# Making the scan's input for four of sixteen units with ScalarE and TensorE instead of VectorE and GpSimd

## The chip, the cores and the metric

The kernel runs on one core of one Trainium2 chip. The core has TensorE (PE in the profile), VectorE (DVE), ScalarE (ACT), GpSimd (POOL), and SyncE (SP), which here only issues DMAs. The metric is the device time of one launch in microseconds. Times are in us unless marked otherwise.

## What is computed

The first of two layers takes `x` of shape (8, 64, 128, 128), runs a small Mamba block along every row and along every column, in both directions, and adds the four results; the second is a residual block of two 3x3 convolutions with batch normalisation. Nearly all the time goes to the Mamba part. Cut to what matters, for one sequence of 128 tokens, 128 inner channels `d` and 16 states `n`:

```python
x, z  = in_w @ seq                                    # 64 -> 128 + 128 channels
u     = silu(causal_conv4(x))                         # four taps along the sequence
dt, B, C = xp_w @ u                                   # 4 + 16 + 16 values per token
delta = softplus(dt_w @ dt + dt_b)
h[d, n] = exp(delta[d] * A[d, n]) * h[d, n] + (delta[d] * u[d]) * B[n]    # per token, in order
y[d]  = sum_n h[d, n] * C[n] + u[d] * D[d]
out   = out_w @ (y * silu(z))
```

The line with `h` is the heavy one: 128 x 16 recurrences for every sequence and direction, so 2048 per token, against 128 lanes in an engine.

## The kernel before

**Groups and units.** The work is cut into 512 groups (8 images, rows then columns, 32 groups each; a group is four sequences, 512 tokens). The recurrences of a group are cut into 16 units. A unit is one direction `d`, one set of four states `ng`, and one half of the channels: 32 channels x 4 states on the 128 partitions, and two channel quarters x 512 tokens along the free axis, 128 x 1024 in all. `where(r)` gives direction, state set and half of unit `r`. For every unit:

- `decay` (L360): ScalarE writes exp(A * delta), two ACTIVATEs of 128x512, into one of two PSUM tiles, `dA0` for even units and `dA1` for odd ones. So a decay can only start when the scan two units earlier has read the same PSUM tile.
- `drive` (L369): delta*u*B, a 128x1024 product. For 11 units VectorE makes it from `du` and `pb`, a PSUM tile in which TensorE has spread B over the partitions (`b_rows`, L353); for the five units in `GPS` GpSimd makes it, from a copy of B fetched by DMA (`b_tile`).
- `scan` (L377): VectorE runs the recurrence along the tokens, in the tile `s`.
- `weigh` (L386): GpSimd multiplies by C.
- `add_up` (L399): TensorE sums over the states into PSUM, four units later.

`s` comes from a pool of eight tiles. `pb`, `bp` and `zp` share one PSUM bank (tag `b`); `cp`, `dp`, `op` and others share one two-bank slot (tag `pt`).

**The order.** No scheduler moves anything: the loop over `s` at the end of the function writes every engine's instruction order by hand, and each engine runs its own queue in that order. One turn of the loop is one unit `r`. Into these turns the loop lays, piece by piece, `prepare` for the next group: four taps of the convolution as matmuls (L237 for rows, L243 for columns), `u` (Silu, L268), `dp` (L275), `bp` and its copy `bc` (L280, L285), softplus (L290), `du` on VectorE and `dl` on ScalarE (L302, L304, and L306, which overwrites each sequence's first or last token), then DMAs that write `du` and `dl` to memory and read them back in the units' layout (`replicate`, L328). Silu and softplus each need another ScalarE table than Exp, so every group loads tables four times. At fixed turns come `gate` (`y`, L412), `emit` (the output product and its copy), and, for the previous image, `normalize` and the first convolution `conv1`.

All DMAs of this part are issued from SP's queue in one order. Images are held whole in SBUF (`xt`); columns are read out of it by a ScalarE copy (L255).

Of the kernel before, what the change touches and what calls it, by code (L numbers as in the profile page):

```python
# [15 lines left out]
P = 128  # L16
# [4 lines left out]
SEQ = N // W  # L21
NCH = W // SEQ
# [7 lines left out]
GPS = (2, 5, 9, 12, 15)  # L30
# [3 lines left out]
def tile_mamba2d_then_resblock(ctx: ExitStack, tc: tile.TileContext, x, par, gn, p_w, o_w, new_p, bn, cst, out):  # L34
# [32 lines left out]
    with tc.tile_pool(name="prep", bufs=2) as prep, tc.tile_pool(name="prep_ps", bufs=2, space=PSUM) as prep_ps:  # L67
        iv = ident.rearrange("p (c n) -> p n c", n=4)
# [3 lines left out]
        for o, p in enumerate(par):  # L72
# [6 lines left out]
            wc = const.tile([P, 2, NTAP, P], F32, name=f"wc{o}")  # L79
            wz = const.tile([P, 2, P], F32, name=f"wz{o}")  # L80
            nc.vector.memset(wc, 0.0)
            nc.vector.memset(wz, 0.0)
            for hf in range(2):
                h = slice(hf * C, (hf + 1) * C)
                for j in range(NTAP):
                    nc.vector.tensor_mul(wc[h, hf, j, :], inw[h, 0:P], cw[h, j, :])
                nc.vector.tensor_copy(wz[h, hf, :], inw[h, P : 2 * P])
# [13 lines left out]
            wb = const.tile([P, NG, 32, 4], F32, name=f"wb{o}")  # L101
            for g in range(NG):
                nc.vector.tensor_copy(
                    wb[:, g], xpT[:, 4 + 4 * g : 8 + 4 * g].unsqueeze(1).to_broadcast([P, 32, 4])
                )
# [3 lines left out]
            av = p["A_log"].rearrange("(q c) (g n) -> q g c n", c=32, n=4)  # L109
# [12 lines left out]
            for hf in range(2):  # L122
# [7 lines left out]
                    wc=wc, wz=wz, wd=wd, wb=wb.rearrange("p g c n -> p (g c n)"), wbc=xpT[:, 4:], A=A, wo=wo,  # L130
# [75 lines left out]
    with ExitStack() as st:  # L206
# [9 lines left out]
        xt = big.tile([P, HH, W], F32, name="xt")  # L216
        xp = big.tile([P, HH, W], F32, name="xp")
        strips = []
        for k in range(2):
            strip = big.tile([P, SEQ + 1, W + 2], F32, name=f"strip{k}")  # L220
            nc.vector.memset(strip, 0.0)
            strips.append(strip)
        far = big.tile([P, SEQ], F32, name="far")
        nc.vector.memset(far, FAR)

        def load_image(b, k):

            rows = slice(k * (HH // 8), (k + 1) * (HH // 8))
            nc.sync.dma_start(out=xt[:, rows, :], in_=x[b].rearrange("p (h w) -> p h w", w=W)[:, rows, :])

        def project(ps, lhsT, g, s, start, stop):

            ps = ps.rearrange("p (q t) -> p q t", t=W)
            if g["o"] == 0:
                hf, r = divmod(SEQ * g["i"], HH)
                lo, hi = max(s, 0), W + min(s, 0)
                nc.tensor.matmul(  # L237
                    ps[:, :, lo:hi], lhsT[hf], xt[:, r : r + SEQ, lo - s : hi - s], start=start, stop=stop
                )
                return  # L240
            for hf in range(2):
                lo, hi = max(hf * HH + s, 0), min((hf + 1) * HH + s, W)
                nc.tensor.matmul(  # L243
                    ps[:, :, lo:hi], lhsT[hf], g["xc"][:, :, lo - s - hf * HH : hi - s - hf * HH],
                    start=start and hf == 0, stop=stop and hf == 1, skip_group_check=True,
                )

        def prepare(g, before):
# [3 lines left out]
            if g["o"] == 1:  # L252
                g["xc"] = work.tile([P, SEQ, HH], F32, name="xc", bufs=1)
                i = SEQ * g["i"]
                nc.scalar.copy(g["xc"], xt.rearrange("p h w -> p w h")[:, i : i + SEQ, :])  # L255
            yield
            cp = psm.tile([P, 2, N], F32, name="cp", tag="pt")
            for d in range(2):
                for s in range(NTAP):
                    j = NTAP - 1 - s  # L260
                    project(
                        cp[:, d, :], [w["wc"][:, 0, j, :], w["wc"][:, 1, j, :]], g,
                        s if d == 0 else -s, s == 0, s == NTAP - 1,
                    )
                    if s % 2:
                        yield
# [10 lines left out]

            bp = psa.tile([P, N], F32, name="bp", tag="b")
            for d in range(2):
                nc.tensor.matmul(  # L280
                    bp[2 * NS * d : 2 * NS * (d + 1), :], w["wbc"], u[:, d, :], start=True, stop=True,
                    skip_group_check=True,
                )
            bc = work.tile([4 * NS, N], F32, name="bc", tag="tok", bufs=3)
            nc.scalar.copy(bc, bp[0 : 4 * NS, :])  # L285
            bd = scratch.tile([2 * NS, 2, N], F32, name="bd")
            nc.sync.dma_start(out=bd.rearrange("n d t -> d n t"), in_=bc)
            g["bd"] = bd
# [11 lines left out]

            du = work.tile([P, 2, N], F32, name="du", tag="nat")
# [3 lines left out]
            for d, edge in enumerate((0, W - 1)):  # L305
                nc.scalar.copy(dl[:, d, :].rearrange("p (s t) -> p s t", t=W)[:, :, edge], far)  # L306
            keep(1, du)
            keep(0, dl)
            yield
            replicate(g, 0, 0)  # L310
            yield
            replicate(g, 1, 0)
            yield
            replicate(g, 0, 1)
            yield
            zp = psa.tile([P, N], F32, name="zp", tag="b")
            project(zp, [w["wz"][:, 0, :], w["wz"][:, 1, :]], g, 0, True, True)
            g["sz"] = work.tile([P, N], F32, name="sz")
            nc.scalar.copy(g["sz"], zp)
            replicate(g, 1, 1)  # L320
            yield

        def replicate(g, half, d):

            for k, what in enumerate(("dl", "du")):
                t = rep.tile([P, 2, N], F32, name=what, bufs=5)
                src = g["dd"][k, d, :, 2 * half : 2 * half + 2, :].rearrange("c q t -> c (q t)")
                nc.sync.dma_start(  # L328
                    out=t.rearrange("p q t -> p (q t)"), in_=src.unsqueeze(1).to_broadcast([32, 4, 2 * N])
                )  # L330
                g[what, half, d] = t

        def where(r):

            ng, k = divmod(r, 4)
            return k % 2, ng, k // 2

        def c_rows(g, r):
# [4 lines left out]
            nc.sync.dma_start(out=t, in_=src.partition_broadcast(32))  # L343
            g["c", ng, d] = t

        def b_tile(g, r):

            half, ng, d = where(r)
            t = rep.tile([P, N], F32, name="bt", bufs=3)
            nc.sync.dma_start(out=t, in_=g["bd"][4 * ng : 4 * ng + 4, d, :].partition_broadcast(32))  # L350
            g["bt", r] = t
# [8 lines left out]
        def decay(g, r):  # L360

            half, ng, d = where(r)
            dA = g["dA", r] = psa.tile([P, 2, N], F32, name=f"dA{half}")
# [5 lines left out]
        def drive(g, r):  # L369
# [3 lines left out]
            engine, b = (nc.gpsimd, g.pop(("bt", r))) if r in GPS else (nc.vector, g["pb"])  # L373
            engine.tensor_mul(s, g["du", half, d], b.unsqueeze(1).to_broadcast([P, 2, N]))  # L374
            g["s", r] = s

        def scan(g, r):  # L377
            half, ng, d = where(r)
            a = g.pop(("dA", r)).rearrange("p j t -> p (j t)")
            s = g["s", r].rearrange("p j t -> p (j t)")  # L380
            if d == 0:
                nc.vector.tensor_tensor_scan(s, a, s, 0.0, ALU.mult, ALU.add)  # L382
            else:
                nc.vector.tensor_tensor_scan(s[:, ::-1], a[:, ::-1], s[:, ::-1], 0.0, ALU.mult, ALU.add)  # L384
# [29 lines left out]
        def emit(g):  # L414

            o, i, w = g["o"], g["i"], wt[g["o"]]
            op = psm.tile([P, 2, N], F32, name="op", tag="pt")[:, 0, :]
# [97 lines left out]

        PREP = range(14)
# [3 lines left out]
        LOAD = (2, 4, 6, 8)  # L522
# [8 lines left out]
        def fetch(s):  # L531

            for k in range(10):
                r = (s + k) % UN
                if 0 <= s + k < total and r in GPS and k == {GPS[0]: 9, GPS[1]: 4}.get(r, 7):
                    b_tile(*at(s + k))
                if 0 <= s + k < total and r % 2 == 0 and k == {0: 7, 4: 4}.get(r, 5):
                    c_rows(*at(s + k))

        def ahead(r):  # L540

            return 2 if r == GPS[0] else 3

        with tc.manual_schedule():
            for k in range(8):
                load_image(0, k)
            for _ in prepare(gs[0], None):
                pass
            for s in range(-9, 0):
                fetch(s)  # L550
            decay(*at(0))
            b_rows(*at(0))
            drive(*at(0))
            for s in range(total + UN):
                n, r = divmod(s, UN)
                live = n < len(gs)
                prev = gs[n - 1] if n else None
                if r == 0:
                    for _ in pieces:
                        pass  # L560
                    pieces = prepare(gs[n + 1], gs[n]) if n + 1 < len(gs) else iter(())
                if s + 1 < total:
                    decay(*at(s + 1))
                    if (s + 1) % UN not in GPS:
                        drive(*at(s + 1))
                for k in (2, 3):
                    if s + k < total and (s + k) % UN in GPS and ahead((s + k) % UN) == k:
                        drive(*at(s + k))
                if live:
                    scan(*at(s))  # L570
                    weigh(*at(s))
                if r == LAG - 1 and prev:
                    gate(prev)
                if s == total - 1:
                    nc.scalar.activation(gs[n]["sz"], gs[n]["sz"], AF.Silu)
                if s % 2 == 0 and s + 2 < total:
                    b_rows(*at(s + 2))
                if r in CONV and n % PER > 6 or r >= CONV[0] and n % PER == 6:
                    next(conv3, None)
                if r in PREP:  # L580
# [177 lines left out]
```

## Time and profile before

| | |
|---|---|
| median of three runs | 27018.82 us (27011.33 to 27033.64) |
| the profiled execution, its own time | 27039.83 us |
| span of its profile | 27038.1 us |
| VectorE busy | 25627.1 us, 95% of the span |
| GpSimd busy | 25129.4 us, 93% |
| TensorE busy | 19439.9 us, 72% |
| ScalarE busy | 17413.3 us, 64% |
| DMA queues, mean rate | 180 GB/s |
| mean granted TensorE clock | 0.876 |

Busy time is the time in which an engine has some instruction in flight. Neighbouring instructions overlap a little, so their durations add up to more than the time they occupy: on VectorE a product lasts 1196 ns by its mean and the next instruction starts about 1.11 us after it. Where instructions follow closely, the distance between starts is the honest price, and the timeline view gives it. "Idle before" in a group's line is the time in which the engine did nothing just before such an instruction, followed by what ended it.

### The profile page before, as it was taken

How to read it: one execution, taken by the hardware profiler on the slowest of the kernel's cores; microseconds unless marked ns; L12 is line 12 of the kernel's file. 1: busy time of each engine (PE TensorE's matmuls, PEld its weight loads, DVE VectorE, ACT ScalarE, POOL GpSimd, SP SyncE). 2: the span in 40 equal slices, each digit the busy share in tenths (PEclk: the TensorE clock that was granted, in tenths of full speed). 3: DMA queues.
4: the chain of work that ended last, by engine and by line, in shares of the span. 5: the costliest groups of instructions: out<-in, count | busy, mean ns of one | idle time of the engine just before them, and what ended most of it. 6: DMA issues, size and time to landing. Idle time of an engine off the chain costs nothing.

```text
span 27038.1 us, 228528 instructions
## 1 busy us (share of the span) xinstructions
PE 19439.9 (72%) x65580; PEld 6680.4 (25%) x65580; DVE 25627.1 (95%) x15633; ACT 17413.3 (64%) x23982; POOL 25129.4 (93%) x10916
## 2 busy tenths in 40 slices
PE   5677777777777777777777777777777777777776
PEld 1222222222222222222222222222222222222232
DVE  8999999999999999999999999999999999999942
ACT  5666666666666666666666666666666666666632
POOL 7999999999999999999999999999999999999930
PEclk8888888888988889888898888988888888988888
DMA  5554555555555555555555555555555555555545
GB/s 181 174 179 172 185 189 184 176 173 186 192 181 175 173 189 192 180 172 173 193 188 177 175 178 193 184 178 174 177 199 179 180 172 182 198 176 179 171 141 188
DMA packets 2165508, 4870.74 MB, mean 180 GB/s; under 512 B 265856, under 2 KB 413456, under 8 KB 2148368
## 3 DMA queue, kind: packets, MB, share of 16 engines
q1 hardware_dynamic: 2143648, 4754.51, 51.8%
q10 hardware_dynamic: 15984, 68.06, 0.9%
q0 software_dynamic: 4608, 33.56, 0.3%
q8 instruction: 517, 8.47, 0.1%
q14 instruction: 751, 6.15, 0.1%
HBM read 4115.52 MB, written 738.98 MB: 180 GB/s over the span
## 4 chain that ended last, share of the span: by engine, by line
DVE 35%; PE 22%; issue 20%; DMA 10%; ACT 10%; SPq 2%; POOL 1%; DVEq 0%; POOLq 0%; ACTq 0%
DVE s L374 15%; DMA du<-dd 9%; DVE s L384 8%; DVE s L382 8%; PE pb L357 6%; ACT dA L365 5%; PE yp L405 5%; PE dp L275 3%; PE cps L667 2%; DVE du L302 2%; PE op L423 1%; PE op L418 1%; PE bp L280 1%; DVE y L412 1%; ACT xp L436 1%
## 5 line engine op out<-in xcount | busy, mean ns | idle before, releaser
L389 POOL TENSOR_TENSOR s<-s,c 128x1024 f32<-128x1024 f32 x8192 | 19136.2, 2362 | 677.1 <-DVE s L384 309.6
L365 ACT ACTIVATE dA<-dl,A 128x512 f32<-128x512 f32 x16384 | 11265.2, 691 | 6399.1 <-DVE s L384 3848.6
L357 PE MATMUL pb<-u,wb 128*128 128x512 f32 x8192 | 5429.6, 750 | 6527.7 <-DVE s L374 5829.9
L384 DVE TENSOR_TENSOR_SCAN s<-dA,s 128x1024 f32<-128x1024 f32 x4096 | 9278.0, 2275 | 15.7 <-POOL s L374 2.5
L382 DVE TENSOR_TENSOR_SCAN s<-dA,s 128x1024 f32<-128x1024 f32 x4096 | 9274.8, 2274 | 0.0
L374 DVE TENSOR_TENSOR s<-du,pb 128x1024 f32<-128x1024 f32 x5632 | 6736.8, 1196 | 168.9 <-DMA du<-dd 100.8
L374 POOL TENSOR_TENSOR s<-du,bt 128x1024 f32<-128x1024 f32 x2560 | 6061.9, 2368 | 142.9 <-DMA bt<-bd 140.8
L405 PE MATMUL yp<-s,fold 128*32 128x512 f32 x32768 | 5170.7, 708 | 5.1 <-POOL s L389 5.1
L357 PEld LDWEIGHTS pb<-u,wb 128*128 128x128 f32 x8192 | 1517.7, 218 | 9607.2 <-issue 3926.7
L237 PE MATMUL cp<-xt,wc 128*128 128x512 f32 (+3 forms) x4096 | 2017.6, 616 | 101.3 <-DMA xt<-x_h 76.9
L243 PE MATMUL cp<-xc,wc 128*128 128x256 f32 (+3 forms) x8192 | 2065.5, 397 | 0.0
L243 PEld LDWEIGHTS cp<-xc,wc 128*128 128x128 f32 x8192 | 1584.7, 199 | 1030.8 <-issue 459.6
L405 PEld LDWEIGHTS yp<-s,fold 128*32 128x32 f32 x32768 | 691.0, 116 | 3773.0 <-issue 1930.8
L365 ACT ACT_TABLE_LOAD x1030 | 1321.5, 1283 | 18.2
L237 PEld LDWEIGHTS cp<-xt,wc 128*128 128x128 f32 x4096 | 764.9, 197 | 1402.0 <-issue 1242.3
L275 PE MATMUL dp<-u,wd 128*128 128x512 f32 x2048 | 1048.9, 638 | 1.2 <-ACT u L268 1.2
L395 PE MATMUL yp<-u,dg 128*128 128x512 f32 x2048 | 963.7, 593 | 1.7 <-DVE y L412 1.7
L696 POOL DMA_DIRECT2D out<-cc x32 | 17.2, 537 | 980.7 <-ACT cc L695 980.7
L436 ACT COPY xp<-op 64x256 f32<-64x256 f32 x512 | 318.2, 621 | 943.2 <-PE op L423 940.2
L495 PE MATMUL cps<-strip,w 128*128 128x512 f32 x1536 | 782.5, 638 | 47.9 <-DMA strip<-x_d 39.4
L418 PE MATMUL op<-y,wo 128*128 128x512 f32 x1024 | 808.7, 882 | 0.8 <-DVE y L412 0.8
L667 PE MATMUL cps<-xp,w 128*128 128x512 f32 x1536 | 675.3, 598 | 8.3 <-ACT xp L655 7.5
(109 smaller groups left out, 10041.2 us busy)
## 6 DMA issues: line engine op xcount, KB each, us to landing
dl<-dd SPq DMA_DIRECT2D x2048, 512.0 KB
du<-dd SPq DMA_DIRECT2D x2048, 512.0 KB
c<-bd SPq DMA_DIRECT2D x4096, 256.0 KB
bt<-bd SPq DMA_DIRECT2D x2560, 256.0 KB
dd<-du SPq DMA_DIRECT2D x2048, 128.0 KB
dd<-dl SPq DMA_DIRECT2D x2048, 128.0 KB
bd<-bc SPq DMA_DIRECT2D x512, 128.0 KB
c_d<-cs SPq DMA_DIRECT2D x256, 256.0 KB
```

The source lines that it names most:

```text
L237: nc.tensor.matmul(ps[:, :, lo:hi], lhsT[hf], xt[:, r : r + SEQ, lo - s : hi - s], start=start, stop=stop)
L243: nc.tensor.matmul(ps[:, :, lo:hi], lhsT[hf], g["xc"][:, :, lo - s - hf * HH : hi - s - hf * HH], start=start and hf == 0, stop=stop and h ...
L275: nc.tensor.matmul(dp[:, d, :], w["wd"], u[:, d, :], start=True, stop=True)
L357: nc.tensor.matmul(pb, wt[g["o"]]["wb"][:, P * ng : P * (ng + 1)], g["u"][:, d, :], start=True, stop=True)
L365: nc.scalar.activation(dA[:, j, :], g["dl", half, d][:, j, :], AF.Exp, scale=wt[g["o"]]["A"][:, 2 * half + j, ng : ng + 1])
L374: engine.tensor_mul(s, g["du", half, d], b.unsqueeze(1).to_broadcast([P, 2, N]))
L382: nc.vector.tensor_tensor_scan(s, a, s, 0.0, ALU.mult, ALU.add)
L384: nc.vector.tensor_tensor_scan(s[:, ::-1], a[:, ::-1], s[:, ::-1], 0.0, ALU.mult, ALU.add)
L389: nc.gpsimd.tensor_mul(s, s, c.unsqueeze(1).to_broadcast([P, 2, N]))
L405: nc.tensor.matmul(g["yp"][32 * q : 32 * (q + 1), :], fold, s[:, j, :], start=False, stop=r == UN - 2, skip_group_check=True,)
L418: nc.tensor.matmul(op, w["wo"].rearrange("p h c -> p (h c)"), g["y"], start=True, stop=o == 0)
L667: nc.tensor.matmul(ps[:, j, :].rearrange("p (r w) -> p r w", w=W), w2[:, blk, kw, :], xp[:, r : r + SEQ, kw : kw + W], start=(kw == 0 and ...
```

## The change

**Order and kinds.** A table `ORDER` gives each of the 16 units its state set, direction and kind. Eight are V (drive on VectorE), four G (drive on GpSimd), four T. Halves still alternate with the unit's number. Units of the same state set and direction share one `pb` (four `b_rows` to a group instead of eight) or one B tile (two `b_tile`s instead of five).

**T units** (4, 7, 12 and 15). Four transposes turn `du` of direction 0 so that tokens lie on the partitions (`duT`), and four small products give B in the same layout (`BT`). `spread` then multiplies: for each state set (2 or 3) and each sequence, four ScalarE activations of 128x128, each with one column of `BT` as its per-partition scale, fill a tile `X`; 32 such activations to a group. `turn` brings the result back with eight TensorE transposes of 128x128 into the PSUM tile `dA0` or `dA1` of that unit. The decay of a T unit goes to an `s` tile in SBUF instead, one to three turns ahead (`EARLY`), and the scan takes its factor from `s` and its input from PSUM.

**Taps.** The image is stacked on the partitions twice, shifted by one token, so that one product does two taps: four matmuls of 128x512 to a group for rows and columns alike, and one for `zp`.

**Columns.** Instead of the whole image, blocks of 32 columns are loaded; a ScalarE copy picks four columns, and DMAs lay them into the stack.

**Layout and places.** The partition order in a unit becomes state-major instead of channel-major, in the constants and in the DMA patterns alike. Within `prepare`, `bp`, `bc` and the `bd` write come later (with `du` and `dl`), and `zp` comes first. All else in the computation is as it was.

```diff
-GPS = (2, 5, 9, 12, 15)
+ORDER = (
+    (0, 0, "V"), (0, 0, "V"), (1, 0, "G"), (1, 0, "G"), (2, 0, "T"), (0, 1, "V"), (0, 1, "V"), (2, 0, "T"),
+    (1, 1, "V"), (1, 1, "V"), (2, 1, "G"), (2, 1, "G"), (3, 0, "T"), (3, 1, "V"), (3, 1, "V"), (3, 0, "T"),
+)
...
+        def spread(g, ng, q):
+            t = g["X", ng, q] = work.tile([P, NQ, 4, 32], F32, name="X", bufs=4)
+            for n in range(4):
+                k = 8 * q + 4 * (ng - TG) + n
+                nc.scalar.activation(
+                    t[:, :, n, :], g["duT"][:, q, :].rearrange("p (q c) -> p q c", c=32), AF.Copy,
+                    scale=g["BT"][:, k : k + 1],
+                )
...
         def decay(g, r):
             half, ng, d = where(r)
-            dA = g["dA", r] = psa.tile([P, 2, N], F32, name=f"dA{half}")
+            if ORDER[r][2] == "T":
+                dA = g["s", r] = unit.tile([P, 2, N], F32, name="s")
+            else:
+                dA = g["dA", r] = psa.tile([P, 2, N], F32, name=f"dA{half}")
...
+        def turn(g, r):
+            half, ng, d = where(r)
+            dB = g["dB", r] = psa.tile([P, 2, N], F32, name=f"dA{half}")
+            for j in range(2):
+                for q in range(SEQ):
+                    nc.tensor.transpose(
+                        dB[:, j, W * q : W * (q + 1)],
+                        g["X", ng, q][:, 2 * half + j, :, :].rearrange("p n c -> p (n c)"), ident,
+                    )
...
+        EARLY = {2: 4, 3: 7, 10: 12, 12: 15}
+        SPREAD = {14: [(2, 0)], 15: [(2, 1)], 0: [(2, 2)], 1: [(2, 3)], 6: [(3, 0)], 7: [(3, 1)], 10: [(3, 2), (3, 3)]}
+        AHEAD = {15: 3, 0: 3, 7: 3, 8: 3}
+        ROWS = {14: 0, 3: 5, 6: 8, 11: 13}
...
+                kind = ORDER[(r + 1) % UN][2]
+                if kind == "T" and live:
+                    turn(*at(s + 1))
+                if g := after if r >= 14 else this:
+                    for k in SPREAD.get(r, ()):
+                        spread(g, *k)
+                if r in EARLY and live:
+                    decay(this, EARLY[r])
+                if kind != "T" and s + 1 < total:
+                    decay(*at(s + 1))
+                if kind == "V" and s + 1 < total:
+                    drive(*at(s + 1))
+                if r in AHEAD and s + AHEAD[r] < total:
+                    drive(*at(s + AHEAD[r]))
                 if live:
-                    scan(*at(s))
-                    weigh(*at(s))
+                    scan(this, r)
+                    weigh(this, r)
```

## The prediction, made before the changed kernel ran

> **What bounds the kernel now.** I read the page's busy times and costliest groups first, then the `y` instructions (one to a group), then the timeline of one row group, engine by engine. From the page:
>
> ```profile
> PE 19439.9 (72%) x65580; PEld 6680.4 (25%) x65580; DVE 25627.1 (95%) x15633; ACT 17413.3 (64%) x23982; POOL 25129.4 (93%) x10916
> ...
> L389 POOL TENSOR_TENSOR s<-s,c 128x1024 f32<-128x1024 f32 x8192 | 19136.2, 2362 | 677.1 <-DVE s L384 309.6
> L365 ACT ACTIVATE dA<-dl,A 128x512 f32<-128x512 f32 x16384 | 11265.2, 691 | 6399.1 <-DVE s L384 3848.6
> ...
> L384 DVE TENSOR_TENSOR_SCAN s<-dA,s 128x1024 f32<-128x1024 f32 x4096 | 9278.0, 2275 | 15.7 <-POOL s L374 2.5
> ...
> L374 DVE TENSOR_TENSOR s<-du,pb 128x1024 f32<-128x1024 f32 x5632 | 6736.8, 1196 | 168.9 <-DMA du<-dd 100.8
> L374 POOL TENSOR_TENSOR s<-du,bt 128x1024 f32<-128x1024 f32 x2560 | 6061.9, 2368 | 142.9 <-DMA bt<-bd 140.8
> ```
>
> VectorE never waits for its scans (15.7 us in all) and hardly for its products: it is the bound, GpSimd just below. ScalarE idles 6399 us before its decays, waiting for scans, 12.5 us to a group. From the `y` line:
>
> ```profile
> L412 DVE TENSOR_TENSOR y<-yp,sz x512: 655/661/692, 188.7 to 25914.2; 128x512 f32<-128x512 f32 x171
> ```
>
> Head 188.7, 511 periods of (25914.2 - 188.7)/511 = 50.34, tail 1124. VectorE's timeline gives the prices:
>
> ```profile
> 9999.27 1.19 DVE L374 TENSOR_TENSOR s<-du,pb 128x1024 f32<-128x1024 f32 x1
> 10000.38 2.28 DVE L382 TENSOR_TENSOR_SCAN s<-dA,s 128x1024 f32<-128x1024 f32 x1
> 10002.58 1.19 DVE L374 TENSOR_TENSOR s<-du,pb 128x1024 f32<-128x1024 f32 x1
> ```
>
> From start to start a product takes 1.11 and a scan 2.20 (`du` 1.12 and `y` 0.58 in the same view). A row group is 16 x 2.20 + 11 x 1.11 + 1.12 + 0.58 = 49.11; the other 1.23 of the period are statistics of columns and convolution, the wait for the column copy (228.8 us in the view of waits, 0.45 a group), image changes. ScalarE's prices, in its timeline:
>
> ```profile
> 9999.38 1.42 ACT L365 ACTIVATE dA<-dl,A 128x512 f32<-128x512 f32 x2 [1.36 <-DVE s L382]
> 10000.82 1.28 ACT L268 ACT_TABLE_LOAD   x1
> 10002.11 1.11 ACT L268 ACTIVATE u<-cp,conv_b 128x1024 f32<-128x1024 f32 x1
> 10003.12 0.62 ACT L270 ACTIVATE sz<-sz 128x512 f32<-128x512 f32 x1
> 10003.64 0.81 ACT L454 ACTIVATE xp<-xp,b_gn,s_gn 128x512 f32<-128x512 f32 x1
> 10004.47 1.28 ACT L365 ACT_TABLE_LOAD   x1
> 10005.76 2.75 ACT L365 ACTIVATE dA<-dl,A 128x512 f32<-128x512 f32 x4
> ```
>
> By starts: a decay 1.44, a table 1.29, `u` 1.01. The first line also shows that a decay starts 0.11 after the scan two units earlier is done.
>
> **What the Trainium skill says.** "ScalarE: Activation LUTs", section "What ACT_TABLE_LOAD costs": an activation takes 186 ns + 0.833 ns per element, each pointer operand adds 93 ns, neighbours overlap by 93 ns. With a pointer scale and 512 elements that is 705; the trace has 691, so I trust it. A `spread` (128 elements, pointer scale) is then an estimated 186 + 93 + 107 = 386 ns, 0.29 from start to start. "TensorE: Matmul & The Clock Gate", "Part 4: PE-mode transpose": about 275 ns for one 128x128 transpose inside a kernel; no run here shows one yet. The same page, "Part 1: The HAM clock gate", says that TensorE's clock halves after a few us of idling; here the `pb` pair takes 1.12 or 2.08:
>
> ```profile
> 10017.29 2.08 PE L357 MATMUL pb<-u,wb 128*128 128x512 f32 x2 [5.92 <-DVE s L374]
> ...
> 10022.78 1.12 PE L357 MATMUL pb<-u,wb 128*128 128x512 f32 x2 [0.32 <-DVE s L374]
> ```
>
> **The change part by part.** VectorE loses three products: 3 x 1.11 = 3.33 a group, to 45.78. GpSimd loses one drive: 20 x 2.34 = 46.8 against 49.1. A T scan swaps which input is in PSUM; I take the same 2.20 (a recurrence paced by its elements), bounds 2.1 and 2.4. TensorE loses four `b_rows` (4 x 1.12) and more than half of the taps, and gains 36 transposes at 0.1 to 0.4, taken as 0.2: in sum no more work than before, so only its waits count. ScalarE gains 32 spreads (32 x 0.30 = 9.6 a group) and two copies (0.48 and some 0.15); T decays write SBUF and lose the wait of the second half for the first, 1.26 instead of 1.44. DMAs: three B tiles fewer, two to four small stack transfers more, column blocks in pieces; engines at a mean share near 53%, all needed a group later. SP's C tile for unit 5 waits at turn 15 for GpSimd's unit 15, and what is behind it (C of unit 8, the stack) is wanted six turns later: nothing. Sharing `dA0`/`dA1` between decays and transposes adds no PSUM but puts a T unit's transposes behind the scan two units earlier.
>
> ScalarE's 9.6 seem to fit in its 12.5 of idling. They don't, because of where they stand. In the changed program ScalarE's queue, from the decay of unit 6 (which waits for scan 4, whose transposes sit in `dA0`) to the decay of unit 11, is fixed. By starts:
>
> decay 6: 1.44; table, `u`, `sz`: 1.29 + 1.01 + 0.64; eight spreads 2.40; table 1.29; decays 8 and 9 2.77; table, softplus, table: 1.29 + 1.11 + 1.29; decay 10 1.44; `dl` 1.04, edges 0.20, `bc` 0.48; eight spreads 2.40; decay 12 (T, ahead of time) 1.26; decay 11 1.42. Sum 22.8, with the start 22.9; 18.1 of it are not spreads.
>
> In that stretch VectorE has scans 5 to 10, drives 6, 8 and 9, and `du`: 6 x 2.20 + 3 x 1.11 + 1.12 = 17.65. So scan 11 must wait 22.9 - 17.65 = 5.2 us for its decay (a part of it, under 1, already at scan 10). Nothing else covers it: scan 11 stands in order on VectorE, and drive 13, scan 12 and GpSimd's unit 11 stand behind it.
>
> The other stretch, from scan 11 to the end of the next group's scan 4, is VectorE's: 10 x 2.20 + 5 x 1.11 + 0.58 = 28.13. ScalarE's work there, 7 decays, 3 T decays, 16 spreads and copies, is near 21 and keeps up. But `b_rows` stands in TensorE's queue behind `turn`: for drive 0, transposes start after scan 13, take 8 x 0.2 = 1.6, then `pb` 1.12 to 2.08 (after the long wait mostly cold) and two hand-overs of 0.1, about 3.4, while VectorE is back after one scan, 2.20: 1.2 late. Drive 5, behind turn 4, has 2.78 (scan, `y`) and is late only when cold: 0.2 on average. (Drive 8 is late too, inside the first stretch, where it costs nothing; without that cover 1.2.)
>
> A group: 22.9 + 28.13 + 1.4, plus `normalize` in a quarter of the groups, 0.83 in the first stretch, 0.2; plus 1.23 - 0.45 = 0.8 of rest: 53.4. Total 188.7 + 511 x 53.4 + 1124 = 28,600 against this profile's 27,039.83; the median shown is 21 less, so 28,580; I say 28,600, 5.8% slower.
>
> **The rivals.** (1) *Faster*: the spreads issue far closer together, and TensorE's turns are never late. For it, the two edge copies of four elements stand 0.1 apart; against it, a pointer scale and 124 more elements. At 0.1 the first stretch is 18.1 + 1.6 = 19.7, a group 19.7 + 28.13 + 1.0 = 48.8, in all 26,260. It decides below a spacing of about 0.19; at 0.2 a group is 50.4, all 27,080: *no change*. (2) *TensorE is late*: transposes at 0.4, clock mostly halved. Drive 0 waits 3.2 + 2.08 + 0.2 - 2.2 = 3.3, drive 5 2.7, and the third set of spreads, which needs the fifth transpose of turn 7, 1.1: 59 a group, 31,400. Against it: 72% busy shrinks rather than grows, and only a quarter of the `pb` pairs were slow. (3) *GpSimd bounds*: would need ScalarE's stretch not to bind; 46.8 is hidden under 53, and this is where (1) at its best would stop: 47.3 a group with the rest of 0.5, 25,480.
>
> **How the numbers follow.** Likeliest, 0.78: ScalarE's stretch with spreads at 0.28 to 0.33 and TensorE waits of 0 to 2.8: 51.7 to 55.4 a group, 27,750 to 29,600. Rival 2 or something between: 0.09. Spacing at 0.2 with no TensorE waits, no change: 0.04. Rivals 1 and 3: 0.09, what I may have misread in the order included. Range for 8 in 10: 27,500 to 29,650. A difference under 0.2% can't be told from none here. Faster 0.08, no change 0.03, slower 0.89.
>
> **What would show it.** Right: VectorE busy falls to about 84%, ScalarE rises above 80%; the scan lines show some 2500 us of idling ended by ScalarE's decays, 4 to 5 us once a group; `drive` shows 500 to 700 us ended by TensorE's `pb`; period of `y` near 53. Wrong: spreads under 0.2 apart; VectorE waiting first for transposes or for GpSimd; scan 11 on time because ScalarE's queue ran ahead in a way that I take as impossible.

## The result, and the profile after

The changed kernel takes 42,207.11 us (median of four runs, 42,178.35 to 42,219.23); the kernel before, run beside it, 27,026.23 us. The ratio is 1.5615 (95% interval 1.5588 to 1.5642). The forecast of 28,600 us had the sign right and the size wrong by 13,600 us.

From the page of the kernel before, the DMA shares (tenths of the 16 DMA engines' time in 40 slices of the span):

```profile
DMA  5554555555555555555555555555555555555545
```

From the page of the changed kernel, its busy times and DMA shares, and then the groups that answer to those shown of before:

```profile
PE 20805.6 (49%) x75308; PEld 8396.9 (20%) x75308; DVE 24254.4 (57%) x14093; ACT 22302.2 (53%) x41390; POOL 23999.2 (57%) x10404
DMA  3233233332333323333233333333333333333325
...
L421 ACT ACTIVATE dA<-dl,A 128x512 f32<-128x512 f32 x12288 | 8464.3, 689 | 13900.3 <-DMA dl<-dd 8084.0
L430 DVE TENSOR_TENSOR s<-du,pb 128x1024 f32<-128x1024 f32 x4096 | 4973.1, 1214 | 13684.5 <-DMA du<-dd 12489.5
L454 DVE TENSOR_TENSOR_SCAN s<-dA,s 128x1024 f32<-128x1024 f32 x4096 | 9199.7, 2277 | 2337.2 <-ACT dA L421 2244.8
...
L430 POOL TENSOR_TENSOR s<-du,bt 128x1024 f32<-128x1024 f32 x2048 | 4828.2, 2358 | 8917.4 <-DMA bt<-bd 8700.0
```

No engine is busy for more than 57% of the span. The forecast's own signs are there: the scans (L454) idle 2337 us, almost all of it ended by ScalarE's decays. But beside them VectorE idles 12,490 us before its drives until `du` is back from memory, ScalarE 8084 us until `dl` is back, and GpSimd 8700 us until `bt` is back. DMA is what is late. Yet its mean share is three tenths, *less* than the five tenths of before, and fewer bytes are moved: 4604 MB against 4871.

The `y` line, one instruction to a group, gives the period:

```profile
L482 DVE TENSOR_TENSOR y<-yp,sz x512: 662/665/691, 240.3 to 41082.2; 128x512 f32<-128x512 f32 x171
```

The period, from the first start to the last, is (41082.2 - 240.3)/511 = 79.93 us against 50.34. So 29.6 us of each group is new, where the forecast had 3.1.

What a late, idle DMA looks like is seen in SP's own queue. The timeline of the DMA issues while a group's `dl` and `du` are fetched, first of the kernel before, then of the changed one (start, time in the queue, what is issued):

```profile
10022.22 0.54 SPq L328 DMA_DIRECT2D dl<-dd  x1
10022.79 0.60 SPq L328 DMA_DIRECT2D du<-dd  x1
10023.51 0.54 SPq L328 DMA_DIRECT2D dl<-dd  x1
10024.09 1.22 SPq L328 DMA_DIRECT2D du<-dd  x1
```

```profile
15009.89 4.81 SPq L381 DMA_DIRECT2D dl<-dd  x1
15014.79 4.77 SPq L381 DMA_DIRECT2D du<-dd  x1
15019.65 7.22 SPq L395 DMA_DIRECT2D c<-bd  x2
15026.98 9.63 SPq L272 DMA_DIRECT2D xs<-xc  x4
```

The same transfers, of the same 512 KB, hold SP's queue for 4.8 us here instead of 0.6. (Over the whole run the four issues of `du` in a group take 0.8, 4.8, 2.5 and 4.8 us by their medians, against 0.6 to 0.7 before.) Even the small `xs<-xc`, which has nothing to do with the layout, takes 2.4 us a piece: it stands in the same congestion.

The packet records of the trace say why. A packet of 4096 bytes takes the same time in both kernels, 159 ns by its median (2048 bytes: 84 ns). What differs is how many packets of 4096 bytes are in flight at once: before, most of the time 13 to 17 (exactly 16 in 41% of the time that has any); after, hardly ever more than 4 (exactly 4 in 52%, more in 5%). Counted together with those of 2048 bytes, exactly 4 are in flight in 74% of that time. The large transfers, all of them together, use four of the 16 DMA engines.

That is the layout. In the change the partitions of a unit became state-major, and the DMA patterns followed. The first experiment takes this back; its edit of the patterns, cut, with `-` for the changed kernel:

```diff
 # replicate: dl and du
-                    out=..., in_=src.unsqueeze(0).to_broadcast([4, 32, 2 * N])
+                    out=..., in_=src.unsqueeze(1).to_broadcast([32, 4, 2 * N])
 # c_rows and b_tile
-            nc.sync.dma_start(out=t, in_=src.unsqueeze(1).to_broadcast([4, 32, N]))
+            nc.sync.dma_start(out=t, in_=src.partition_broadcast(32))
```

State-major, the memory side of the pattern starts with a dimension of size 4; channel-major, with one of size 32. The Trainium skill says what this does: in "DMA: Bandwidth & Descriptors", section "Why a DMA increments its semaphore by 16 and not by 1", a transfer takes the largest number of DMA engines, up to 16, that divides the size of the outermost dimension (leaving out those of size 1) on both sides, and the section "Rules for kernel authors" warns of a leading broadcast of a few copies, which is the case of `dl` and `du`. With 128 partitions on one side and 4 on the other that is 4; with 32 it is 16. The trace agrees: 4 packets in flight against 16.

The price can be estimated from these packets. A group fetches eight tiles of `dl` and `du`, 128 packets of 4096 bytes each: on four engines 8 x 32 x 0.159 = 40.7 us. Eight tiles of `c` with 2048-byte packets are 8 x 32 x 0.084 = 21.5, two of `bt` 5.4. Together 67.6 us on the four engines that also carry their part of everything else, for a period of 79.9; on sixteen engines the same would be 16.9 by this estimate.

### The profile page after: what moved, and what is told of

Its sections match the earlier page's. It is cut to its first block, busy times and chain, and to the rows that moved or that the text cites. A ratio compares the mean times of both kernels' runs of the same rounds, so it can differ in the third digit from the quotient of the medians.

```text
span 42198.5 us, 268927 instructions
## 1 busy us (share of the span) xinstructions
PE 20805.6 (49%) x75308; PEld 8396.9 (20%) x75308; DVE 24254.4 (57%) x14093; ACT 22302.2 (53%) x41390; POOL 23999.2 (57%) x10404
## 5 line engine op out<-in xcount | busy, mean ns | idle before, releaser
L421 ACT ACTIVATE dA<-dl,A 128x512 f32<-128x512 f32 x12288 | 8464.3, 689 | 13900.3 <-DMA dl<-dd 8084.0
L430 DVE TENSOR_TENSOR s<-du,pb 128x1024 f32<-128x1024 f32 x4096 | 4973.1, 1214 | 13684.5 <-DMA du<-dd 12489.5
L454 DVE TENSOR_TENSOR_SCAN s<-dA,s 128x1024 f32<-128x1024 f32 x4096 | 9199.7, 2277 | 2337.2 <-ACT dA L421 2244.8
L439 PE MATMUL dA<-ident,X 128*128 128x128 f32 x16384 | 3158.5, 356 | 11050.6 <-DVE s L454 11027.6
L371 ACT ACTIVATE X<-duT,BT 128x128 f32<-128x128 f32 x16384 | 5054.3, 388 | 4623.0 <-PE dA L439 4623.0
L439 PEld LDWEIGHTS dA<-ident,X 128*128 128x128 f32 x16384 | 2596.2, 186 | 13066.6 <-DVE s L454 11952.2
L452 DVE TENSOR_TENSOR_SCAN s<-dA,s 128x1024 f32<-128x1024 f32 x2048 | 4574.6, 2275 | 928.2 <-POOL s L430 898.6
L452 DVE TENSOR_TENSOR_SCAN s<-s,dA 128x1024 f32<-128x1024 f32 x2048 | 4668.0, 2279 | 0.0
L290 PE MATMUL cp<-xs,wc 128*128 128x512 f32 x4096 | 2850.7, 833 | 234.3 <-ACT cs L571 234.3
L410 PE MATMUL pb<-u,wb 128*128 128x512 f32 x4096 | 2959.0, 815 | 0.0
L421 ACT ACTIVATE s<-dl,A 128x512 f32<-128x512 f32 x4096 | 2718.1, 712 | 9.7
```

What stands on the lines that cost most here:

```text
L290: nc.tensor.matmul(cp[:, d, :].rearrange("p (q t) -> p q t", t=W), w["wc"][:, d, k, :], g["xs"][:, :, t : t + W], start=k == 0, stop=k == 1,)
L371: nc.scalar.activation(t[:, :, n, :], g["duT"][:, q, :].rearrange("p (q c) -> p q c", c=32), AF.Copy, scale=g["BT"][:, k : k + 1],)
L410: nc.tensor.matmul(pb, wt[g["o"]]["wb"][:, P * ng : P * (ng + 1)], g["u"][:, d, :], start=True, stop=True)
L421: nc.scalar.activation(dA[:, j, :], g["dl", half, d][:, j, :], AF.Exp, scale=wt[g["o"]]["A"][:, 2 * half + j, ng : ng + 1])
L439: nc.tensor.transpose(dB[:, j, W * q : W * (q + 1)], g["X", ng, q][:, 2 * half + j, :, :].rearrange("p n c -> p (n c)"), ident,)
L452: nc.vector.tensor_tensor_scan(s, a, b, 0.0, ALU.mult, ALU.add)
```

## The experiments

**Layout alone, DMA patterns alone.** Theory A: the four DMA engines make the whole difference from the forecast, and what is left is the forecast's stretch of ScalarE. Rivals: the rest of the change (spreads, transposes, the new order, the small stack transfers) is dearer than forecast; or the traffic is too many transfers rather than too few engines. Four kernels tell these apart; of the second, third and fourth there is one run each.

First, the changed kernel with channels outermost again, in constants, `X` tiles and patterns (the diff above, with `[P, NQ, 32, 4]` for `X` and `t[:, :, :, n]` for what a spread writes). All else of the change stays.

> Theory A (transfers on few DMA engines): the changed kernel's DMA patterns that fill dl, du, c and bt now begin with a dimension of 4 on the memory side where they began with 32 or a 32-fold broadcast, and each such transfer runs on 4 DMA engines instead of 16. This kernel is the changed one with the partition order inside a unit turned back to channel-major, and with it those four patterns; all else of the change stays. A expects the 4 KB packets to run up to 16 at a time again, the waits for dl, du and bt to vanish, and the time to fall from 42,200 to what was forecast without this effect, 28,600 (27,500 to 29,650), with scan 11 waiting some 5 us for ScalarE's decay in every group. Theory B (the T units and the new order cost the time, on TensorE and ScalarE): above 38,000. Theory C (the many small packets of stacks and column blocks choke SP's queue): above 38,000.

Measured: 29,178.26 us, ratio to before 1.0793 (1.0775 to 1.0811). The page and the view of waits of this kernel:

```profile
PE 19174.7 (66%) x75308; PEld 8069.5 (28%) x75308; DVE 24070.8 (82%) x14093; ACT 22499.5 (77%) x41390; POOL 24065.7 (82%) x10404
```

```profile
DVE s L454 <- ACT dA L421: 2275.3, 574, 4.8
...
DVE s L430 <- PE pb L410: 902.5, 877, 1.8
DVE s L430 <- issue: 832.1, 545, 2.0
```

The long DMA waits are gone, and 13,029 us with them. In front of the scans stands what the forecast named, ScalarE, with 2275 us; in front of the drives, TensorE's `pb`.

Second, the reverse: the kernel *before* with nothing but the state-major layout, in its constants (`[P, NG, 4, 32]` for `wb`) and the three DMA patterns.

> The kernel before with state-major partitions and DMA patterns, and nothing else of the change. A: a group moves 8 transfers with 32 packets of 4 KB on each of 4 engines (32 x 0.159 = 5.1 us) and 13 with 32 packets of 2 KB (2.7 us): 76 us a group where the period was 50.3, so 39,000 to 44,000. B and C: within 1% of 27,020.

Measured: 45,186.65 us, above what was expected. This kernel fetches five B tiles a group instead of two, another 3 x 2.7 = 8 us on the four engines, and its period is 85.73 us against the changed kernel's 79.93. The expectation had counted these tiles; its 76 us fall short of the period by 10, as the 67.6 above do by 12. Exactly four packets of 4096 bytes are in flight in 87% of the time that has any. The chain that ended last, as shares of the span:

```profile
DMA dl<-dd 27%; DMA du<-dd 24%; DVE s L374 6%; PE pb L357 5%; DVE s L382 4%; PE yp L405 4%; DMA bt<-bd 3%; ACT dA L365 2%; DVE s L384 2%; PE dp L275 2%; PE cps L667 1%; PE cp L243 1%; SPq L328 1%; PE cp L237 1%; DVE du L302 1%
```

Half of that chain is the fetching of `dl` and `du`. The layout with its patterns, with none of the spreads, is enough.

Third and fourth: the changed kernel as it is, state-major, but each of these transfers issued as four of 32 partitions, so that both sides begin with 32; once for all four kinds (`dl`, `du`, `c` and `bt`), once for `dl` and `du` only. The edit for `dl` and `du`:

```diff
-                nc.sync.dma_start(out=t.rearrange("p q t -> p (q t)"), in_=src.unsqueeze(0).to_broadcast([4, 32, 2 * N]))
+                for n in range(4):
+                    nc.sync.dma_start(out=t[32 * n : 32 * (n + 1)].rearrange("p q t -> p (q t)"), in_=src)
```

> The changed kernel, state-major as it is, with every transfer to dl, du, c and bt issued as four transfers of 32 partitions, so that no pattern begins with 4. A: the engines are all used; 74 issues of about 0.5 us a group take 40 to 46 us of SP's queue, which still fits, so 28,000 to 31,000. B: above 38,000. C: above 38,000, rather more than before, since SP issues more.

> Only the transfers to dl and du are issued as four; c and bt still begin with 4. A: of the 68 us a group on the four engines, 41 (8 x 5.1) go, 27 for c and bt stay and fit under a period of 53: 28,000 to 31,500, close to the kernel with all transfers split. B and C: above 38,000.

Measured: 29,170.45 us with all split, 30,855.74 us with `dl` and `du` only. With all split, four times as many issues move the same bytes and the time is that of the channel-major kernel to 8 us, so it is the number of engines and not the order of the data, nor the number of transfers. In this kernel, as in the channel-major one, exactly four packets of 4096 bytes are in flight in only 3% of the time that has any. `c` and `bt` on four engines are worth 1,685 us by themselves.

**What the other 2,150 us are.** From here on everything is built on the channel-major kernel (29,178 us). Its idle times on VectorE, as means over the groups, by the place in a group: scan 11 4.41, drive 0 1.61, drive 8 1.35, drive 13 0.22, drive 5 0.18, scan 10 0.16; with some crumbs 8.0 us of a period of 54.53. The forecast blamed ScalarE's order for the first and TensorE's order for the drives. ScalarE's part in its timeline, channel-major kernel, from the decay of unit 10 to that of unit 11:

```profile
15003.81 1.42 ACT L421 ACTIVATE dA<-dl,A 128x512 f32<-128x512 f32 x2
15005.16 1.00 ACT L328 COPY dl<-dp 128x1024 f32<-128x1024 f32 x1
15006.19 0.29 ACT L330 COPY dl<-far 128x4 f32<-128x4 f32 x2
15006.39 0.57 ACT L332 COPY bc<-bp 64x512 f32<-64x512 f32 x1
15006.87 2.57 ACT L371 ACTIVATE X<-duT,BT 128x128 f32<-128x128 f32 x8
15009.23 1.31 ACT L421 ACTIVATE s<-dl,A 128x512 f32<-128x512 f32 x2
15010.44 1.40 ACT L421 ACTIVATE dA<-dl,A 128x512 f32<-128x512 f32 x2
```

ScalarE doesn't pause; scan 10 starts at 15005.32 and is over after 2.29, and scan 11 can't start before the last of these lines is done; it starts at 15011.94. The first of two tests puts decay 11 ahead of the spreads and of decay 12 in turn 10:

```diff
+                if r == OUT and s + 1 < total:
+                    decay(*at(s + 1))
                 if g := after if r >= 14 else this:
                     for k in SPREAD.get(r, ()):
                         spread(g, *k)
...
-                if kind != "T" and s + 1 < total:
+                if kind != "T" and r != OUT and s + 1 < total:
                     decay(*at(s + 1))
```

> The changed kernel with channels outermost on the partitions (29,178 us), and in turn 10 ScalarE computes decay 11 before the eight spreads and decay 12 instead of after them. Theory S (the scan of unit 11 waits 4.4 us a group because ScalarE serves the two spreads and decay 12 first): decay 11 comes some 4.8 us earlier and the wait at scan 11 goes; the spreads and decay 12 end 1.4 us later than they did, so scan 12 can't start before the moment at which scan 11 started so far, plus 0: about 2.3 us of the 4.4 is gained a group, 512 x 2.3 = 1,180 us, 27,700 to 28,300 us, and what is left of the wait stands at scan 12. Rival R (ScalarE's total load, not its order, sets the period): within 100 us of 29,178 us, the wait only moves.

Measured: 28,741.26 us, 437 us gained where about 1,180 were expected. The wait at scan 11 fell from 4.41 to 0.85, as the theory said, but 2.9 of the 3.6 were lost again at once, and not at scan 12: drive 13 now waits 3.08 instead of 0.22. Its `pb` stands on TensorE behind the transposes of unit 12, which need the last `X`. (Whether `X` makes them late is for the third kernel below to show.)

The second test puts the `b_rows` of a turn ahead of its transposes:

```diff
+                if r in ROWS and (g := after if r >= 14 else this):
+                    b_rows(g, ROWS[r])
                 if kind == "T" and live:
                     turn(*at(s + 1))
```

(and takes the same two lines out further down).

> The changed kernel with channels outermost (29,178 us), and TensorE computes the B rows (pb) of the V units before the transposes of the same turn instead of after the turn's other TensorE work. Theory P (the waits of drive 0, 1.6 us, and of drive 8, 1.35 us a group, come from TensorE's order alone): both waits go. The one before drive 0 is gained whole; what is gained at drive 8 is lost again at scan 11, which waits for ScalarE: 512 x 1.6 = 820 us, 28,200 to 28,600 us, and the wait at scan 11 grows from 4.4 to about 5.7 us. If both counted: 27,650 us. Rival (the pb wait is that of its PSUM buffer or of ScalarE): within 150 us of 29,178 us.

Measured: 27,803.60 us, 1,375 us gained: 2.69 a group, where 1.6 was expected. By place: drive 0's 1.61; 0.40 at drives 13 and 5, which the expectation had left out; and of drive 8's 1.35 only a half was lost again, as scan 10's wait rose from 0.16 to 0.82 while scan 11's stayed at 4.33. So the wait at drive 8 was covered by ScalarE's stretch only in part. The reason, read from the traces and not tested by a run of its own: that stretch has a hand-over from VectorE in its middle. Decay 9 needs the PSUM tile that scan 7 reads, and scan 7 stands behind drive 8. Over 480 groups of the channel-major kernel ScalarE idles 0.33 us a group ahead of decay 9, which in three groups of four starts 0.1 after the end of scan 7, and it takes 23.55 us from decay 6 to decay 11; with the rows first it doesn't wait there, and the mean is 22.87.

The third kernel of this series has the four spreads of state set 3 in turns 2, 3, 4 and 7 instead of 6, 7 and 10, seven `X` buffers instead of four, and decay 11 first. The fourth is this one with the `b_rows` first as well.

> The changed kernel with channels outermost (29,178 us), decay 11 first in turn 10, seven X buffers instead of four, and the four spreads of state group 3 issued in turns 2, 3, 4 and 7 instead of 6, 7, 10 and 10. Theory S (the place of the spreads makes scan 11 wait): no wait of over 0.5 us a group is left at scans 11 and 12; 512 x 4.4 = 2,250 us is gained, 26,700 to 27,300 us, if no new wait comes up in turns 2 to 8. Rival R (ScalarE's sum of 44 us a group is near the bound wherever its work stands): the wait moves to the scans of units 3 to 9, over 28,300 us.

> The kernel of the run with moved spreads, and the B rows ahead of the transposes in their turn. Theory: with the waits at scans 11 and 12 and at drives 0 and 8 gone, VectorE (45.8 us a group) or GpSimd (24,066 us busy in 512 groups, 47.0 us) bounds the group: period 47.3 to 48.8 us, with 193 us ahead and 1,113 us behind 25,500 to 26,300 us, below the kernel before (27,030 us). Rival R (ScalarE is the bound): over 27,500 us.

Measured: 29,053.10 and 27,250.39 us, both slower than their theories expected. With the spreads out of turn 10 and decay 11 first, scan 11's wait is down to 0.96, but drive 13 waits 2.72, nearly as much as with decay 11 first alone, and scan 3, behind a spread in turn 2, a new 0.88. So the transposes that drive 13's `pb` stands behind were not late because of `X`. In the kernel with moved spreads, the timeline of TensorE in turns 10 and 11, and from that of VectorE the drive that waits:

```profile
15033.32 1.11 PE L343 MATMUL op<-ident,du 128*128 128x128 f32 x4 [5.49 <-ACT dl L328]
15034.36 1.94 PE L475 MATMUL yp<-s,fold 128*32 128x512 f32 x8
15036.23 1.74 PE L487 MATMUL op<-y,wo 128*128 128x512 f32 x2
15037.80 1.04 PE L439 MATMUL dA<-ident,X 128*128 128x128 f32 x8
15038.68 1.02 PE L410 MATMUL pb<-u,wb 128*128 128x512 f32 x2
...
15039.74 1.22 DVE L430 TENSOR_TENSOR s<-du,pb 128x1024 f32<-128x1024 f32 x1 [1.96 <-PE pb L410]
```

TensorE stands still for 5.5 us before the transposes of `du`, because these wait for ScalarE's copy `dl`: they write the PSUM slot (tag `pt`) that it reads. Row sums, the output product, unit 12's transposes and only then `pb` for drive 13 come after, back to back. TensorE is idle for much of a group and still late here. (With the rows first, in the fourth kernel, the unit's transposes come after `pb` and the rest stays ahead of it: 2.11 at drive 13.) The next step builds on the fourth kernel and issues `pb` for unit 13 right behind the transposes of `du`:

```diff
                 next(pieces, None)
+                if r == OUT and live:
+                    b_rows(this, 13)
```

A second kernel, built on this one, puts every decay ahead of its turn's spreads and decay 11 ahead of `dl`.

> The previous kernel (27,250 us), with the B rows of unit 13 issued in turn 10 ahead of that turn's row sums and output products, instead of at the head of turn 11 behind them. Theory Q (drive 13's wait of 2.1 us a group is TensorE's queue: the transposes of delta u wait for ScalarE's copy, and sums, output products and then the B rows stand behind them): the wait goes, 512 x 2.1 = 1,080 us, 26,100 to 26,400 us. Rival R (unit 12's state is late from ScalarE anyway): the wait moves to scan 12, within 150 us of 27,250 us.

> The same, and each turn's decay ahead of its spreads on ScalarE, decay 11 ahead of the copies of delta. Theory: the waits of 0.88 us at scan 3 and 0.87 us at scan 11 go as well; the period is then that of VectorE's own work (45.8 us) or of GpSimd's (46.9 us) with little added, 47.0 to 48.2 us, 25,350 to 26,000 us, faster than the kernel before by 4 to 6%. Rival R: ScalarE (22,517 us busy, 44.0 us a group) now sets the end at some other place, over 26,200 us.

Measured, with `pb` moved: 27,069.54 us (ratio to before 1.0017, 1.0010 to 1.0024), 181 us gained instead of 1,080. As the rival said, the wait moves from drive 13 (now 0.23) to scan 12 (1.68), but not for the rival's reason: unit 12's transposes, not a decay, end it (853 us in all), and these are still behind the output product. The second of the two takes 28,351.69 us. Both waits that it was made for are gone, but waits of 2.3 us at drive 13 and 1.5 at drive 5 are new, and scan 12 waits 1.9. Decay 11 ahead of `dl` makes TensorE's late stretch later still: it idles 3432 us in all for `dl`, against 2814. At drive 5, `pb` waits for ScalarE's copy `sz`, which frees the PSUM bank that `pb` shares with `zp`.

Last, two kernels without the second of these steps. One issues unit 12's transposes in turn 10 behind `pb`, ahead of sums and output product, and decays 15 and 13 ahead of ScalarE's copy of `duT`. The other adds, in turn 2, decay 3 first and the spread behind the copy `sz`:

```diff
                 if r == OUT and live:
                     b_rows(this, 13)
+                    turn(this, 12)
...
+                if r == 2 and live:
+                    for k in SPREAD[2]:
+                        spread(this, *k)
```

> The previous best order (27,070 us) with the transposes of unit 12 on TensorE right behind the B rows of unit 13 in turn 10, ahead of that turn's row sums and output products, and with decays 15 and 13 on ScalarE ahead of the copy of delta u transposed, which waits for the output products. Theory Q (TensorE's queue in turns 10 and 11 holds the transposes up): the waits at scan 12 (1.7 us a group) and drive 13 (0.2 us) go; 512 x 1.9 = 970 us, 26,000 to 26,300 us, faster than before by 3 to 4%. Rival R (the wait moves on to scan 13, as ScalarE's copy waits for products that now end 1 us later): within 200 us of 27,070 us.

> The same, and in turn 2 decay 3 first and the spread behind the copy of the gate, so that neither scan 3 nor the B rows of unit 5 (whose PSUM buffer that copy frees) wait for the spread. Theory: the wait of 0.9 us at scan 3 goes without a new one at drive 5: 512 x 0.88 = 450 us less than the run before it, 25,550 to 25,900 us. Rival: decay 5 now comes 0.7 us later and scan 5 waits for it; the gain is under 150 us.

Measured: 27,066.12 and 26,654.10 us. In the first the wait moved a third time, back to drive 13 (1.40), now ended by the row sums:

```profile
DVE s L430 <- PE yp L475: 717.6, 512, 2.0
```

Drive 13 writes one of the eight `s` tiles, and it is the row sums, now behind the transposes, that give it back. The rest of what was gained at scan 12 is lost in the groups of columns, to a wait that the step before did not have. There a statistics instruction of VectorE waits about 1.1 us for ScalarE's copy of the output product, which now ends later:

```profile
DVE gst L509 <- ACT xp L505: 271.9, 256, 4.1
```

The second gained the 0.9 us at scan 3 that it was meant to gain (412 us) with no new wait of any size. It is the fastest kernel of the study, 26,654.10 us, ratio to before 0.9862 (0.9847 to 0.9876). Its page:

```profile
PE 19062.6 (72%) x75308; PEld 7780.3 (29%) x75308; DVE 24049.2 (90%) x14093; ACT 22432.2 (84%) x41390; POOL 23986.5 (90%) x10404
```

So the change as a whole gains 1.4% with the patterns and the orders put right. Which of its parts (T units, shared `pb`, stacked taps, column blocks) bring this was not tested apart. VectorE's idle places still add up to some 2.5 us a group of rows, most of it in turns 10 to 12, where TensorE has to do five things (two sets of transposes, `pb`, row sums, output product) after one late copy.

One rival was not tested: TensorE's granted clock is 0.80 in the channel-major kernel and 0.84 in the fastest, against 0.88 before, and how much of TensorE's lateness comes from this is open.

## Why the prediction was wrong, and where it was right

**The step that failed** is the sentence on DMAs: "three B tiles fewer, two to four small stack transfers more, column blocks in pieces; engines at a mean share near 53%, all needed a group later." It counted transfers and bytes, and took the mean share as spare room. The change of the access patterns, which the description of the change names, was costed at nothing without asking how many DMA engines the new pattern uses. The runs show that it uses four instead of 16. The runs put that term at 13,030 us (42,207 against 29,178 and 29,170). The forecast's range had no case for it, and no rival named DMA at all. The rule quoted above could have been looked up, but the forecast does not mention the new patterns.

**Without that term** the channel-major kernel can be held against the sum, step by step. It takes 29,178 us, inside the forecast's range; the forecast was 28,600, a period of 53.4 against 54.53.

- VectorE's own work, 45.78 and 0.8 of rest, 46.6: measured 54.53 less 8.0 of waits, 46.5. T scans at 2.20 from start to start were right too (mean duration 2280 ns against 2269 to 2278 of the others).
- ScalarE's stretch: the wait at scans 10 and 11 was forecast at 5.2 and is 4.57; with drive 8's 1.35, which falls into the same stretch, 5.9. The spreads stand 2.36/8 = 0.295 apart in the timeline above, for a forecast of 0.29, taken as 0.30. Whether `X` is written in runs of 32 elements or one element in four changes the mean duration of a spread (388 to 502 ns) but not this spacing (2.35 us for eight in the split kernel).
- "Drive 8 is late too, inside the first stretch, where it costs nothing": wrong by half, as the run with the rows first shows: 0.7 of its 1.35 counted.
- Drive 0 was forecast 1.2 late and is 1.61; drive 5 0.2 and 0.18. Drive 13's 0.22 was not forecast.
- Transposes, taken as 0.2 each with bounds of 0.1 and 0.4: eight take 1.04 to 1.97 us, 0.13 to 0.25. The 275 ns for one that the forecast quotes from the Trainium skill ("TensorE: Matmul & The Clock Gate", "Part 4: PE-mode transpose") are above that; the page gives them for bf16, and these transposes are of f32. Rival 2, TensorE late by its transposes' own length, did not occur.
- The signs named: scans idling some 2500 us behind ScalarE (2245 even in the changed kernel, 2275 in the channel-major one) and `drive` behind `pb` (forecast 500 to 700; 888 in the changed kernel, 902 in the channel-major one and another 832 that the view puts under "issue", which is drive 0) were both seen, next to the one that nobody had named. VectorE at 84% and ScalarE above 80% were not (57 and 53%; 82 and 77% in the channel-major kernel).

So slower was right, for waits that are real and were worth 2,150 of the 15,180 us. But one part of the picture was missing here too. The forecast made ScalarE's stretch the only reason why turns 10 to 12 are long. With most of the wait at scan 11 taken away, by decay 11 first alone and then with the spreads moved too, the kernel was only 437 and 125 us faster than the channel-major one, because TensorE, behind ScalarE's copy `dl`, was late for drive 13 by nearly as much. The forecast's sum has no such term.

## What to carry to other kernels

When an access pattern of a DMA changes, look at the size of its outermost dimension on both sides before counting bytes: a broadcast or a state index of 4 in front kept each transfer here to four of the sixteen engines, and the low mean DMA share was a sign of the trouble and not of spare room. A wait that moves from place to place under reordering can point to a queue with one late input: in several runs here the order behind that input did little more than decide who pays. Where a stall is called hidden inside another engine's stretch, look for a buffer in the middle of the stretch that passes through the stalled engine.

## What the runs showed of the hardware

- A transfer on four DMA engines holds the issuing queue: 4.8 us for one issue of 512 KB, against 0.6, once several are under way. Smaller transfers behind it, with another pattern, are held as well (2.4 us each in the timeline above, 1.4 by the median, against 0.6 in the channel-major kernel).
- Splitting such a transfer in four costs almost nothing here: mostly 1.75 to 1.9 us of SP's queue for four issues in place of 0.5 to 0.6 for one that uses all engines, and a total time within 8 us of that kernel's.
- On ScalarE a write with a step of four elements lengthens an activation of 128 elements from 388 to 502 ns, and the next one starts no later for it.
